# Eight, six and two: a mixture-of-experts kernel whose 16 blocks go through the experts in three groups instead of two

## The chip, the cores and the metric

One core of a Trainium2 chip runs the whole program. The time is device microseconds of one execution; the kernel before has a median of 1375.88 us over 18 runs (1373.22 to 1378.5). A profile is one further execution, with a span of its own.

The engines are named as in the profile: PE is TensorE (PEld its weight loads), DVE is VectorE, ACT is ScalarE, POOL is GpSimd, and SP is the sync engine, which here only issues DMAs.

## What is computed

`x` is 8 sequences of 1024 tokens of 256 numbers, all in float32. Two layers follow each other. The first is an RWKV layer (time mix with a scan over the tokens, then channel mix). The second, which the change is about, sends each token to 4 of 32 experts:

```python
def _L0_ffn_ref(x, expert_sel, keys, values):
    ...
    sel_logits = jnp.einsum('nd,ed->ne', xt, expert_sel)
    gates = jax.nn.sigmoid(sel_logits)
    sel_val, sel_idx = jax.lax.top_k(gates, N_HEADS)
    gate_full = jnp.zeros_like(gates).at[jnp.arange(N)[:, None], sel_idx].set(sel_val)
    scores = jax.nn.relu(jnp.einsum('nd,edf->nef', xt, keys))
    scores = scores * gate_full[:, :, None]
    out = jnp.einsum('nef,efv->nv', scores, values)
    return out.reshape(B, S, -1)
x = L0_attn_x
x = x + _L0_attn_ref(_layernorm(x, axis=-1), L0_attn_ln1_g, ...)
x = x + _L0_ffn_ref(_layernorm(x, axis=-1), L0_ffn_expert_sel, L0_ffn_keys, L0_ffn_values)
return x
```

An expert is a 256x128 matrix, a ReLU and a 128x256 matrix (`N_HEADS` is 4, `E` is 32).

## The kernel before

**Blocks and periods.** The 8192 tokens are 16 blocks of 512, two to a sequence. `period(i)` (L978) is a list of pieces, written out by hand, that works on four blocks at once: the routing of block i-1 (`norm_d`, `apply_d`, `turn_d`, `gates_of`, `rows_of`, `scatter`, `gates_by_row`), the channel mix of block i (`channel`, `channel_end`, which stores the block's result to DRAM as `acc`, L445), the time mix of block i+1, and the load and first norm of block i+2. The loop at L1080 runs periods 0 to 16; in period 16 only the routing of block 15 is left. Between the pieces stand 15 calls of `advance()` (L954).

**Routing.** `gates_of` computes the gates and marks the four largest; `rows_of` gives each token four row numbers in a DRAM buffer `xs` of its group, where each expert has a region of its own. `scatter` puts 16 entries (4 rows of 128 tokens, 4 choices) into the list `waiting`; `post(n)` (L558) issues n of them as indirect DMAs on POOL (L563, `xs<-x,row`, 128 rows each). A helper, `behind_others`, keeps a scatter behind the POOL work written before it.

**Groups.** Blocks are collected into groups, `GROUPS` (L31), before 12 and 4 blocks. When all blocks of a group are routed, its rows can be worked through expert by expert. `expert_group` (L1058) is a generator that does this in small steps beside the periods: `tile_table` counts the rows of each expert and makes a table of tiles; `experts` runs the tiles; `combine` adds the results to the tokens. `advance()` calls `post(1)` and then moves each running generator; the five numbers of a group are its size, the steps to wait before the second half of the table, the tiles per step, the steps between tiles and sums, and the sums per step. A group begins two periods after its last block (L1082), after all that still waits to be scattered is posted at once (L1083). The last group begins after the loop (L1091), and `drain()` calls `advance()` until all is done.

**Tiles.** A tile is 256 rows of one expert; the last 16 tiles of every group are split into two halves of 128 rows for two experts, which is where the partly filled ends of the experts' regions go. So a group of n blocks has `n * 512 * 4 / 256 + 16 = 8n + 16` tiles (`n_tiles`, L148), before 112 and 48. For each tile SP fetches the rows (`xg`, L759), three tiles ahead, five once the periods are over; PE transposes them (`trx`, L794), DVE (in later groups ACT) copies the transposes out (`xgT`, L878) and DVE copies the expert's keys (`key`, L785), PE multiplies by the keys (`ph`, L806), ACT applies the ReLU (`hs`, L884), PE multiplies by the values (`po`, L822), ACT copies that out (`yg`, L888; three buffers, six once the periods are over), and POOL issues two indirect DMAs (`send`, L834, `ys<-yg,to`) that put the rows where their token and choice have their place in DRAM. PE's order is `po` of tile r, `ph` of tile r+2, `trx` of tile r+4.

**Sums.** `combine` handles 128 tokens at a time (a "part", four to a block): SP loads the block's `acc` (`ac`, L901) and gathers 512 KB (`g`, L909), DVE does four multiply-adds (L917), and SP stores the block (L930; the last block part by part, L927). A gather needs every `ys` scatter of its group to have landed. The gathers have two buffers, six once the periods are over; `ac` shares its three buffers (tag `x`) with the blocks that are still under way.

**What sets the order.** A scheduler may move an instruction on its engine where nothing binds it; tiles of a group are pinned to their order, and some norms and loads are kept in program order. Each engine, and each DMA queue, then works through its list in order: SP and POOL stop at an instruction whose input is not there, and everything behind it waits. `clear` fills the front of a group's regions with zeros (two fills of 4224 KB and two of 132 KB on SP's queue); the first is written before the loop, the second after period 0. `load_experts` loads the experts' weights after periods 2 to 5.

Of the kernel before, what the change touches and what calls it, by code (L numbers as in the profile page):

```python
# [27 lines left out]
TS = 256  # L28


GROUPS = ((12, 6, 1.8, 4, 0.8), (4, 4, 1.0, 2, 1.0))  # L31


@with_exitstack
def rwkv_then_routed_experts(
# [43 lines left out]
    groups, first = [], 0  # L79
    for size, *_ in GROUPS:  # L80
        groups.append(list(range(first, first + size)))
        first += size
    assert first == len(blocks)
    group_of = {i: g for g, members in enumerate(groups) for i in members}
# [148 lines left out]
    def transposed(src, c, i, k):  # L233

        ps = ps_a.tile([P, TB], F32, tag="a", name=f"tr_{i}_{k}_{c}")
        for t in range(NT):
            nc.tensor.transpose(ps[:, t * P : (t + 1) * P], src[:, t, c * P : (c + 1) * P], ident)
        return ps
# [109 lines left out]
    def scale_shift(src, i, k):  # L348

        mv = moments(src, i, k)  # L350
        ve = p2.tile([P, NT], F32, tag="ve", name=f"ve_{i}_{k}")
        nc.vector.tensor_scalar(ve, mv[:, :, 1], EPS, None, ALU.add)
        rs = rsqrt(ve, i, k)
        nb = p2.tile([P, NT], F32, tag=f"nb_{k}", name=f"nb_{i}_{k}")
        mine[i][f"{k}_made"] = nc.vector.scalar_tensor_tensor(
            nb, mv[:, :, 0], -1.0, rs, ALU.mult, ALU.mult
        )
        return rs, nb

    def apply(src, dst, rs, nb):  # L360
        for t in range(NT):
            tc.keep_in_program_order(
                nc.scalar.activation(
                    dst[:, t, :D], src[:, t, :], AF.Identity, bias=nb[:, t : t + 1], scale=rs[:, t : t + 1]
                )
            )
# [80 lines left out]
    def norm_d(i):  # L447
        m = mine[i]
        m["d"] = scale_shift(m["x"], i, "d")

    def apply_d(i):
        m = mine[i]
        m["x3"] = p2.tile([P, NT, DX], F32, tag="x3", name=f"x3_{i}")
        apply(m["x"], m["x3"], *m["d"])

    def turn_d(i):
        m = mine[i]
        xT = p3.tile([P, KC, TB], F32, tag="xT", name=f"xT3_{i}")
        for c in range(KC):
            nc.scalar.copy(xT[:, c, :], transposed(m["x3"], c, i, "d"))  # L460
        m["xT3"] = xT

    def gates_of(i):
        m = mine[i]
        xT = m["xT3"]
        ps = ps_a.tile([P, NT, NE], F32, tag="a", name=f"lg_{i}")
        for t in range(NT):
            for c in range(KC):
                nc.tensor.matmul(
                    ps[:, t, :],  # L470
                    xT[:, c, t * P : (t + 1) * P],
                    wsel[:, c, :],
                    start=(c == 0),
                    stop=(c == KC - 1),
                )
        el = p1.tile([P, NT, NE], F32, tag="el", name=f"el_{i}")
        nc.scalar.activation(el, ps, AF.Exp, scale=-1.0)
        nc.vector.tensor_scalar(el, el, 1.0, None, ALU.add)


        ga = p2.tile([P, NT, NE + PAD], F32, tag="ga", name=f"ga_{i}")
        nc.vector.memset(ga[:, :, NE:], -1.0)
        nc.vector.reciprocal(ga[:, :, :NE], el)
        m8 = p2.tile([P, NT, 8], F32, tag="m8", name=f"m8_{i}")
        rp = p1.tile([P, NT, NE + PAD], F32, tag="rp", name=f"rp_{i}")
        for t in range(NT):
            nc.vector.max(m8[:, t, :], ga[:, t, :])
        nc.vector.memset(m8[:, :, TOP:], -1.0)
        for t in range(NT):
            nc.vector.match_replace(rp[:, t, :], m8[:, t, :], ga[:, t, :], -2.0)  # L490
        chosen = p2.tile([P, NT, NE], BF16, tag="chosen", name=f"chosen_{i}")
        nc.vector.tensor_tensor(chosen, ga[:, :, :NE], rp[:, :, :NE], ALU.not_equal)
        m["ga"], m["chosen"] = ga, chosen
# [45 lines left out]
    waiting = []  # L539
    own_names = set()  # L540

    def scatter(i):
        waiting.extend((i, t, k) for t in range(NT) for k in range(TOP))
# [14 lines left out]
    def post(count):  # L558

        for i, t, k in waiting[:count]:  # L560
            m = mine[i]
            g = group_of[i]
            s = nc.gpsimd.indirect_dma_start(  # L563
                out=xs[g],
                out_offset=bass.IndirectOffsetOnAxis(ap=m["row"][:, t, k : k + 1], axis=0),
                in_=m["x3"][:, t, :],
                in_offset=None,
            )
            apart("scatter", g, s)
            behind_others(s)  # L570
        del waiting[:count]

    def gates_by_row(i):

        m = mine[i]
        eq = p2.tile([P, NT, TOP, NE], F32, tag="ek", name=f"eq_{i}")
        gate = keep.tile([P, NT, TOP], F32, name=f"gate_{i}")
        each = [P, NT, TOP, NE]
        nc.vector.tensor_tensor(
            eq,  # L580
            m["key"][:, :, None, :].to_broadcast(each),
            m["k8"][:, :, :TOP, None].to_broadcast(each),
            ALU.is_equal,
        )
        nc.vector.tensor_tensor(eq, eq, m["ga"][:, :, None, :NE].to_broadcast(each), ALU.mult)
        nc.vector.tensor_reduce(gate, eq, AX.X, ALU.add)
        routed[i] = gate
# [363 lines left out]
    total_blocks = len(blocks)  # L951
    background = []

    def advance():  # L954

        post(1)
        for entry in list(background):
            entry[1] += 1.0
            while entry[1] > 0.0:
                try:  # L960
                    entry[1] -= 1.0 / next(entry[0])
                except StopIteration:
                    background.remove(entry)
                    break
# [5 lines left out]
    def beside(stream):  # L970
        next(stream)
        background.append([stream, 0.0])
# [5 lines left out]
    def period(i):  # L978


        do(norm_d, i - 1)
        if i:
            do(mix_wk, i + 1, 0)
        advance()
        do(turn_c, i)
        if i:
            do(mix_vr, i + 1, 0)
        advance()
        do(apply_d, i - 1)
        do(fetch_block, i + 2)  # L990
        do(receptance, i)
        advance()
        do(channel, i, 0)
        if i:
            do(mix_scan, i + 1, 0)
        advance()
        if i:
            do(mix_wk, i + 1, 1)
        do(turn_d, i - 1)
        do(norm_a, i + 2)  # L1000
        advance()
        do(channel, i, 1)
        advance()
        if i:
            do(mix_vr, i + 1, 1)
        advance()
        do(channel, i, 2)
        do(mix_scan, i + 1, 1)
        advance()
        do(gates_of, i - 1)  # L1010
        do(channel, i, 3)
        do(norm_b, i + 2)
        advance()
        do(channel, i, 4)
        advance()
        do(mix_out, i + 1)
        do(norm_c, i + 1)
        advance()
        do(channel, i, 5)
        do(rows_of, i - 1)  # L1020
        do(scatter, i - 1)
        do(turn_b, i + 2)
        advance()
        do(channel, i, 6)
        advance()
        do(channel, i, 7)
        do(gates_by_row, i - 1)
        advance()
        do(apply_c, i + 1)
        do(channel_end, i)  # L1030
        advance()

    STEPS = 16
    norm_a(0)
    norm_b(0)
    turn_b(0)
# [16 lines left out]
    apply_c(0)  # L1053
    mix_scan(1, 0)

    done = set()

    def expert_group(g, wait, tiles, pause, sums):  # L1058

        making = tile_table(g)  # L1060
        next(making)
        for _ in range(wait):
            yield 1.0
        for _ in making:
            pass

        while g and ("tiles", g - 1) not in done:
            yield 1.0
        for _ in experts(g, 0 if g else 4):
            yield tiles  # L1070
        done.add(("tiles", g))
        for _ in range(pause):
            yield 1.0
        while g and ("sums", g - 1) not in done:
            yield 1.0
        for _ in combine(g):
            yield sums
        done.add(("sums", g))

    for i in range(total_blocks + 1):  # L1080
        for g, (size, *pace) in enumerate(GROUPS):
            if i == groups[g][-1] + 2:  # L1082
                post(len(waiting))  # L1083
                beside(expert_group(g, *pace))
        period(i)
        if i + 1 < len(groups):
            clear(i + 1)
        elif 2 <= i < 6:
            load_experts(i - 2)
    blocks_over.append(True)  # L1090
    post(len(waiting))  # L1091
    beside(expert_group(len(groups) - 1, *GROUPS[-1][1:]))
    drain()

# [44 lines left out]
```

## Time and profile before

| what | us |
|---|---|
| median of 18 runs | 1375.88 |
| the profiled execution | 1371.3 |
| its span (the rest lies around it) | 1369.6 |
| PE busy | 1224.6 |
| POOL busy | 636.5 |
| DVE busy | 973.3 |
| ACT busy | 555.9 |
| scatters of rows to `xs` (L563) | 256 of 1000 ns mean |
| scatters of results to `ys` (L834) | 320 of 994 ns mean |
| mean granted TensorE clock | 0.96 |
| bytes moved by DMA | 209.73 MB, mean 153 GB/s |

The span is the time from the first to the last recorded event. [...] "Idle before" an instruction is the time in which its engine did nothing just before it, with what ended that time; "issue" means that nothing that the profile shows was waited for.

### The profile page before, as it was taken

The page shows a single profiled execution, that of the slowest core. Times are in us where ns is not written, and L with a number is a line of the kernel's source. Part 1 is how long each engine was busy: PE and PEld are TensorE (multiplying, and loading weights), DVE is VectorE, ACT ScalarE, POOL GpSimd, SP SyncE. Part 2 cuts the span into 40 slices and gives each one's busy share as a digit, 9 for nine tenths or more (in the row PEclk, how much of TensorE's full clock was granted, in tenths as well). Part 3 has the DMA queues.
Part 4 walks back from the last instruction along what each step waited for, and adds up shares of the span by engine and source line. Part 5 has one row for each costly group of instructions (what it writes and reads, how often), then busy time and mean ns, then how long its engine had stood idle before and what let it go on. Part 6 is the DMA issues. An engine that isn't in the chain of part 4 may idle for free. (4 is left out here: it accounts for less than half of the span.)

```text
span 1369.6 us, 18501 instructions
## 1 busy us (share of the span) xinstructions
PE 1224.6 (89%) x5332; PEld 879.0 (64%) x5332; DVE 973.3 (71%) x3058; ACT 555.9 (41%) x1058; POOL 636.5 (46%) x643
## 2 busy tenths in 40 slices
PE   6999999999999999999999999999998858898800
PEld 2566666666666676666665777878877647676700
DVE  5957878878878879777887765764564645376878
ACT  3354444544544444444544344345343223454400
POOL 2011433432432422523517366677677777777620
PEclk9999999999999999999999999999999989899955
DMA  9900221412401201201203355456566664599999
GB/s 323 342 29 14 87 87 65 152 60 92 152 32 59 91 29 63 91 17 66 85 22 134 101 169 163 141 171 203 165 195 207 192 192 115 216 387 398 347 336 334
DMA packets 119412, 209.73 MB, mean 153 GB/s; under 512 B 17130, under 2 KB 77574, under 8 KB 118800
## 3 DMA queue, kind: packets, MB, share of 16 engines
q1 hardware_dynamic: 89616, 138.71, 32.1%
q0 software_dynamic: 27648, 68.23, 13.5%
q10 hardware_dynamic: 2048, 1.61, 0.4%
q8 instruction: 44, 0.72, 0.2%
q14 instruction: 56, 0.46, 0.1%
HBM read 105.68 MB, written 111.17 MB: 158 GB/s over the span
## 5 line engine op out<-in xcount | busy, mean ns | idle before, releaser
L834 POOL DMA_INDIRECT ys<-yg,to x320 | 318.0, 994 | 146.0 <-issue 56.9
L563 POOL DMA_INDIRECT xs<-x,row x256 | 255.9, 1000 | 83.1 <-issue 63.9
L244 PE MATMUL pj_f<-xT,wkey 128*128 128x512 f32 x512 | 242.2, 596 | 0.8 <-ACT ek L293 0.5
L423 PEld LDWEIGHTS cm<-wval,k 128*128 128x128 f32 x1024 | 194.4, 190 | 73.8 <-issue 49.4
L423 PE MATMUL cm<-wval,k 128*128 128x256 f32 x1024 | 240.4, 379 | 0.1
L806 PE MATMUL ph<-xgT,key 128*128 128x256 f32 (+1 forms) x768 | 173.4, 357 | 36.2 <-ACT hs L884 16.4
L822 PE MATMUL po<-wexp,hs 128*128 x640 | 170.2, 389 | 8.3 <-ACT hs L884 8.1
L371 POOL TENSOR_TENSOR x<-x,xa 128x1024 f32<-128x1024 f32 x16 | 37.7, 2356 | 295.8 <-issue 284.1
L806 PEld LDWEIGHTS ph<-xgT,key 128*128 128x128 f32 x768 | 134.2, 198 | 57.7 <-ACT hs L884 17.0
L878 DVE COPY xgT<-trx 128x512 f32<-128x512 f32 x112 | 76.9, 687 | 128.0 <-PE trx L794 127.7
L917 DVE SCALAR_TENSOR_TENSOR ac<-g,gate,ac 128x256 f32<-128x256 f32 x256 | 121.4, 484 | 44.2 <-DMA g<-ys 39.6
L415 ACT ACTIVATE k<-pj_f 128x512 f32<-128x512 f32 x128 | 76.4, 597 | 186.5 <-PE pj_f L244 186.5
L244 PEld LDWEIGHTS pj_f<-xT,wkey 128*128 128x128 f32 x512 | 92.6, 191 | 71.6 <-issue 66.9
L888 ACT COPY yg<-po 128x512 f32<-128x512 f32 x160 | 93.6, 585 | 89.7 <-DMA ys<-yg,to 89.6
L822 PEld LDWEIGHTS po<-wexp,hs 128*128 128x128 f32 x640 | 113.6, 195 | 25.1 <-ACT hs L884 10.0
L884 ACT ACTIVATE hs<-ph 128x256 f32<-128x256 f32 x160 | 61.9, 387 | 138.3 <-PE trx L794 136.1
L325 DVE RECIPROCAL rw<-rw 128x512 f32<-128x512 f32 x32 | 107.3, 3352 | 1.0
L794 PE MATMUL trx<-ident,xg 128*128 128x128 f32 x640 | 100.4, 280 | 7.7 <-DMA xg<-xs 5.1
L794 PEld LDWEIGHTS trx<-ident,xg 128*128 128x128 f32 x640 | 81.0, 145 | 25.5 <-DMA xg<-xs 7.8
L321 POOL COPY tail<-ek 128x1 f32<-128x1 f32 x16 | 15.7, 982 | 143.5 <-DVE ek L317 141.0
L416 ACT ACTIVATE k<-k 128x512 f32<-128x512 f32 x128 | 80.7, 630 | 4.0
L785 DVE COPY key<-wexp 128x256 f32 x192 | 59.8, 320 | 27.0 <-PE ph L806 12.9
(162 smaller groups left out, 1725.2 us busy)
## 6 DMA issues: line engine op xcount, KB each, us to landing
xg<-xs SPq DMA_DIRECT2D x128, 264.0 KB
g<-ys SPq DMA_DIRECT2D x64, 512.0 KB
xs<-zeros SPq DMA_DIRECT2D x4, 4224.0 KB
xg<-xs SPq DMA_DIRECT2D x64, 132.0 KB
x<-in_x SPq DMA_DIRECT2D x16, 512.0 KB
acc<-x SPq DMA_DIRECT2D x16, 512.0 KB
wexp<-in_w_exp SPq DMA_DIRECT2D x4, 2048.0 KB
ac<-acc SPq DMA_DIRECT2D x16, 512.0 KB
```

Source lines behind the costliest of these rows:

```text
L244: nc.tensor.matmul(ps, w(c), rhs[:, c, :], start=(c == 0), stop=(c == KC - 1))
L325: inverse = nc.vector.reciprocal(rc, rc)
L416: nc.scalar.activation(k2, k2, AF.Square)
L423: nc.tensor.matmul(m["cm"][t // 2][:, t % 2, :], k2[:, t * P : (t + 1) * P], wval[:, f, :], start=(f == 0 and t % 2 == 0), stop=(f == FC - 1),
L563: s = nc.gpsimd.indirect_dma_start(out=xs[g], out_offset=bass.IndirectOffsetOnAxis(ap=m["row"][:, t, k : k + 1], axis=0), in_=m["x3"][:, t ...
L794: nc.tensor.transpose(ps[:, c, j * P : (j + 1) * P], xg[:, j, c * P : (c + 1) * P], ident)
L806: nc.tensor.matmul(ps[:, cols], key[:, c * P : (c + 1) * P], xgT[:, c, cols], start=(c == 0), stop=(c == KC - 1),)
L822: nc.tensor.matmul(ps[:, j, :], hs[:, j * P : (j + 1) * P], wexp[:, bass.ds(e, 1), KC * P :], start=True, stop=True,)
L834: s = nc.gpsimd.indirect_dma_start(out=ys[g], out_offset=bass.IndirectOffsetOnAxis(ap=to[:, j : j + 1], axis=0), in_=yg[:, j, :], in_offse ...
L878: after(move(xgT, trx), signal)
L888: after(nc.scalar.copy(yg, po), signal)
L917: nc.vector.scalar_tensor_tensor(ac, gk, routed[i][:, t, k : k + 1], ac, ALU.mult, ALU.add)
```

## The change

`GROUPS` gets three entries: 8, 6 and 2 blocks, with 80, 64 and 32 tiles and paces of their own. There is a third `clear`, after period 1, and a third tile table. Period 16 is replaced by `closing(15)`, which does the routing of block 15 with three calls of `advance()` instead of 15. A group that begins no longer posts all waiting scatters at once: `expert_group` notes that it has begun, `advance()` then posts two a step while the first waiting entry is of such a group, and the tiles wait until none of the group's is left.

```diff
-GROUPS = ((12, 6, 1.8, 4, 0.8), (4, 4, 1.0, 2, 1.0))
+GROUPS = ((8, 6, 1.1, 4, 0.8), (6, 4, 2.0, 4, 1.0), (2, 1, 1.0, 2, 1.0))
...
     def advance():
 
-        post(1)
+        post(2 if waiting and group_of[waiting[0][0]] in begun else 1)
         for entry in list(background):
...
-    STEPS = 16
+    def closing(i):
+
+        norm_d(i)
+        post(2)
+        advance()
+        apply_d(i)
+        post(2)
+        advance()
+        turn_d(i)
+        gates_of(i)
+        post(2)
+        advance()
+        rows_of(i)
+        scatter(i)
+        gates_by_row(i)
+
...
-    done = set()
+    done, begun = set(), set()
 
     def expert_group(g, wait, tiles, pause, sums):
 
+        begun.add(g)
         making = tile_table(g)
         next(making)
         for _ in range(wait):
             yield 1.0
         for _ in making:
             pass
+
+        while any(group_of[i] == g for i, _, _ in waiting):
+            yield 1.0
 
         while g and ("tiles", g - 1) not in done:
             yield 1.0
...
     for i in range(total_blocks + 1):
         for g, (size, *pace) in enumerate(GROUPS):
             if i == groups[g][-1] + 2:
-                post(len(waiting))
                 beside(expert_group(g, *pace))
+        if i == total_blocks:
+            closing(i - 1)
+            break
         period(i)
...
     blocks_over.append(True)
-    post(len(waiting))
     beside(expert_group(len(groups) - 1, *GROUPS[-1][1:]))
     drain()
```

## The prediction

> **What bounds the kernel now.** I read the page's forty slices first, then the stretches, then the waits and the order of time where one stretch hands over to the next.
>
> ```profile
> PE   6999999999999999999999999999998858898800
> POOL 2011433432432422523517366677677777777620
> DMA  9900221412401201201203355456566664599999
> ```
>
> A slice is 34.24 us. Up to about 1027 us PE is full; after that it has gaps, POOL stays at 6 to 7 tenths, and DMA fills up at the end. The stretches say what the 7 means (columns: busy time and count of PE, PEld, DVE, ACT, POOL, then TensorE clock, DMA share, GB/s):
>
> ```profile
> 411.00:445.00 34.00, 34.00 (x131) 22.00 (x130) 27.98 (x77) 16.76 (x30) 9.36 (x11) 1.00 0.17 59
> 1061.00:1096.00 35.00, 28.05 (x143) 22.91 (x141) 22.30 (x106) 9.36 (x22) 26.99 (x27) 0.95 0.66 193
> 1233.00:1267.00 34.00, 27.20 (x152) 21.79 (x151) 23.29 (x84) 16.20 (x36) 26.03 (x26) 1.00 1.05 399
> 1335.00:1370.00 35.00, 0.00 (x0) 0.00 (x0) 27.90 (x62) 0.00 (x0) 0.00 (x0) 0.50 0.90 327
> ```
>
> 27 scatters in 35 us is one per 1.30 us, of which 1.00 is busy. The waits of POOL show that the rest isn't a wait for anyone:
>
> ```profile
> POOL ys L834 <- issue: 27.1, 89, 0.3
> POOL xs L563 <- issue: 8.5, 28, 0.3
> ```
>
> (1013 to 1268 us; total, times, longest.) 0.3 us lies between any two scatters, so 1.28 us a scatter is POOL at its limit, and a tile (two scatters) costs 2.56 us there. On PE a tile costs less:
>
> ```profile
> 1038.11 1.03 PE L822 MATMUL po<-wexp,hs 128*128 x4
> 1038.97 1.03 PE L806 MATMUL ph<-xgT,key 128*128 128x256 f32 x4
> 1039.83 0.60 PE L794 MATMUL trx<-ident,xg 128*128 128x128 f32 x4
> 1040.27 1.03 PE L822 MATMUL po<-wexp,hs 128*128 x4
> ```
>
> From one `po` to the next 2.165 us: 0.87 for `po`, 0.87 for `ph`, 0.43 for `trx`. So the kernel is PE-bound while blocks run, POOL-bound from there to the last scatter (1310.6 us), and then sums only: 1311.9 to 1369.6, 57.7 us.
>
> ```profile
> 515.62 0.37 SPq L445 DMA_DIRECT2D acc<-x  x1
> 568.44 0.37 SPq L445 DMA_DIRECT2D acc<-x  x1
> 1182.68 6.15 DMA g<-ys
> 1341.69 24.80 DVE L917 SCALAR_TENSOR_TENSOR ac<-g,gate,ac 128x256 f32<-128x256 f32 x52 [0.15 <-DMA g<-ys]
> ```
>
> The first two (SP's queue) give the period without tiles, 52.82 us. The third (the chain of waits) prices a gather. The last is the final stretch of sums, 13 parts in 24.8 us: 1.91 a part.
>
> **Part 1, the sizes.** 8n+16 tiles a group makes 80+64+32 = 176 for 160: 16 tiles more, or 34.6 us on PE (16 x 2.165) and 41.0 on POOL (32 x 1.28). The third fill (8.9 MB) follows the second on SP; two took SP from 12.0 to 64.5 us, so this one ends near 91, before block 0's store at 93.2 and the load at 101.3 that are behind it, and the DMA share from 68 to 103 us was 0.10. It costs 0; without that cover, up to 5. Also at 0, behind POOL's limit in part 4: the third table (three small products and some 45 small DVE operations), `xgT` on ACT for 96 tiles in place of 48 (ACT then has 0.585 + 0.385 + 0.585 = 1.56 us a tile against POOL's 2.56), and `closing`, whose 12 lost steps move tiles of group 1 behind block 15's routing but not their number; with POOL not full, each of the three would cost PE a few us at a group's start, as at 1054.3 us, where PE sat 2.9 us before block 15's gates.
>
> **Part 2, to the end of group 0.** In the changed kernel's instruction order all 80 tiles of group 0 stand inside periods 9 to 14, none before. Block 8's store is unchanged at 515.6. Six periods are 316.9, 80 tiles 173.2: block 14's store at 1005.7. Group 0's start cost something before: the period from 727.5 to 808.5 us took 81.0, where 52.8 and 12 `trx`, 10 `ph`, 9 `po` (21.7) explain 74.5. I take 4 of those 6.5 us (bounds 0 and 6.5), since the burst of scatters is gone. POOL has room: 16.5 tiles a period and 16 row scatters are 49 x 1.28 = 63 us, with the other POOL operations of a period (2.4 for x, 2 x 1.3 for the tails) 68 of 88.5. A store is 2.3 us behind PE's last product, and the last `po` of group 0 stands 1.7 before that end: call it T = 1006.
>
> **Part 3, group 1's start.** Here the "two by two" doesn't happen. Group 0's last tile ends a period before group 1 begins, so in POOL's order there is nothing left to put between: its last two scatters, two rows of block 12 and all 16 of block 13 stand in one run, 20 x 1.28 = 26 us, to T+27. They land (2.4 us, `xs<-x,row` rows of the chain), SP fetches (753.63 to the first `trx` at 756.57: 2.9), so `trx` of tile 0 starts at T+33. PE has period 15 to do until then, but not freely: DVE's first sums of group 0 stand in its order before the end of the table and of block 14's norm. They wait for the gather of rows just scattered (two scatters, landing, 6.15: T+12) and for another that needs its buffer (T+20); PE then has 11 us to the tile. It arrives at T+33 too.
>
> Behind it SP's order is: fetch 0, a gather, fetch 1, a load, fetch 2, two gathers, the store of block 0, **the load of block 2, which waits until that store has landed**, fetch 3. From T+30: gather 6, sums 1.9 and what DVE has between, T+40; store 5 (1.5 us for 524 KB at 340 GB/s, 11.94 the longest `out<-ac` of the chain): T+46; fetch 3 at T+49. In PE's order the fourth `trx` is ahead of the first `po`; that, and ACT's copy of 0.6, bring POOL its first result scatter at T+51. POOL stands idle for 24 us. Without the wait of SP it would be T+41 (7.8 us of PE work and the copy after `trx`), idle 14; with the longest store T+58, idle 31. Before, POOL crossed its group change without such a gap, because tiles of group 0 were still queued behind the burst.
>
> [...]
>
> **Part 4, POOL to its last scatter.** 96 tiles are 192 scatters, blocks 14 and 15 add 32. Undisturbed 1.28; with sums beside them, 65 between 1183.1 and 1267.8 us, 1.32. At 1.31 they take 293 us; I add 7, about the two waits before 1274 and 1278 us in the trace (4.9 and 1.2). From T+51 that is T+351 = 1357, where before it was 1311.9. Here the two by two does happen, for block 15, and is worth nothing: POOL is full with or without the mixture. PE, from T+33, needs 208 us for 96 tiles and some 20 for the rest of period 15 and block 15's routing: T+261, so POOL covers it, and would cover waits of PE in the closing chain of several tens of us.
>
> [...]
>
> **Part 5, the end.** Before, 26 gathers were still to come when PE ended; now group 1's 24 parts run beside group 2's 32 tiles and 8 parts remain. Landing 2.5, a gather 6, eight parts 15.3, last store 3.1 (last sum 1366.5, end 1369.6): 27. I take 31, for what group 1 leaves over; bounds 25 and 42.
>
> **The sum.** 1357 + 31 = 1388 of span, 18 more than 1369.6: POOL's last scatter comes 45 later (41 for added scatters; the rest is the gap, less what was done earlier), the end is 27 shorter. The profiled run lies 4.6 below the median, so 1375.9 + 18 = **1394 us**. Lower bounds together (no start loss, idle 14, 1.30 a scatter, end 25): 1002 + 41 + 291 + 25 = 1359, or 1365 on the median's scale; upper bounds 1008 + 58 + 305 + 42 = 1413, or 1419.
>
> **Rivals.**
> - *The gap closes (20%).* If group 0's tiles in fact lag on POOL, so that its run of scatters covers the table and the fetch, POOL never idles: 1006 + 244 x 1.29 + 31 = 1352, 1358 on the median's scale, faster. For it: the trace crosses the change at 1130 us with PE idle for 16.4 us and POOL full. Against: 20 us of slack a period in part 2. It decides from a gap below some 6 us.
> - *DMA takes over at the end (12%).* A part moves 0.79 MB (gather, load, store) and a tile 0.53. Group 2's phase has one part a tile, 36 MB: at 387 GB/s 93 us, against 82 on POOL; with SP's waits for stores 10 to 20 us more: 1404 to 1414. For it: 1233 to 1267 at 399 GB/s. Against: POOL was full there all the same.
> - *Shorter end and added tiles cancel (8%).* With the gap near 10: 1374 to 1379.
> - The change not doing what it says is part 3, and already in the forecast.
>
> The forecast has 60%. Likeliest range 1380 to 1408. About 0.2% (2.8 us) is what can be told from no change. Faster has the first rival and a little, 21%; within 0.2% 7%; slower 72%. The range goes from the first rival's 1358 to the second's 1414.
>
> **What would show it.** Right: 352 result scatters; block 14's store near 1010; 16 row scatters without a break just after, then POOL idle over 15 us; last scatter near 1357; about 30 us from there to the end. Wrong: a gap of a few us, scatters at more than 1.4 us, an end beyond 45, or tiles that stretch the periods by more than 2.165 each.

## The result, and the profile after

| | before | after |
|---|---|---|
| median, us | 1375.64 (50 runs) | 1392.75 (8 runs, 1390.86 to 1394.25) |
| ratio to before | | 1.0125, 95% interval 1.0114 to 1.0136 |
| span of the profiled execution | 1369.6 | 1390.6 |
| block 14's store, block 15's store | 919.59, 1013.55 | 1010.67, 1091.29 |
| scatters not yet begun at block 15's store | 225 | 204 |
| end of POOL's last scatter | 1311.8 | 1368.6 |
| from there to the end | 57.8 | 22.1 |

The changed kernel is 17 us slower. The last four rows are the account used for every run below: a span is block 15's store (up to there PE sets the pace), plus the scatters that are left times the time of one, plus the end. Before it is 1013.6 + 225 x 1.325 + 57.8, after it is 1091.3 + 204 x 1.359 + 22.1. The store comes 77.7 us later, POOL's part is 20.9 shorter, the end 35.8 shorter: 21.0 us of span. That is 4 us more than the medians differ by, because the profiled execution of the kernel before was one of its quicker ones (1371.3 us, its median 1375.6); the one after was at its median (1392.3). Spans of single executions, in this section and the next, are to be read with that much room.

The forty slices of the page, now 34.77 us each:

```profile
PE   6999999999999999999999999999978888796881
POOL 2011343333333334356565555555653777777762
DMA  9990231421411212244434435333167999754995
```

POOL's 3 in the slice at 1043 us, between a 5 and the 7s, is the hole of the prediction's part 3. Its two edges, in POOL's order of time (start, duration, operation, and in brackets the idle time before it and who ended that):

```profile
1031.30 0.96 POOL L563 DMA_INDIRECT xs<-x,row  x1 [0.30 <-issue]
1061.09 1.00 POOL L834 DMA_INDIRECT ys<-yg,to  x1 [28.83 <-ACT yg L888]
```

The run of row scatters ends at 1032.3 us, and POOL is idle for 28.83 us until a result of group 1 is ready. The chain that ended last goes through the same stretch. Its longest pieces there (start, duration):

```profile
1007.80 2.42 DMA ys<-yg,to
1010.25 4.13 DMA g<-ys
1017.07 7.27 DMA g<-ys
1028.99 5.10 PE pj_f L244 x8
1034.86 6.11 DMA xg<-xs
1043.14 6.12 DMA out<-ac
1049.84 4.00 DMA xg<-xs
1055.06 1.81 PE po L822 x4
```

Read downwards: group 0's last result lands, two gathers for its sums follow, then products for block 15's mix on PE, a fetch of group 1's first rows, **the store of block 0's result**, and only behind it one more fetch. SP's order shows the hold:

```profile
1010.67 0.40 SPq L445 DMA_DIRECT2D acc<-x  x1
...
1043.14 0.43 SPq L930 DMA_DIRECT2D out<-ac  x1
1049.28 0.37 SPq L901 DMA_DIRECT2D ac<-acc  x1
1049.84 0.97 SPq L759 DMA_DIRECT2D xg<-xs  x2
```

The load of block 2 starts 6.1 us after the store, when that has landed (6.12 in the chain), and the fourth fetch of rows stands behind it. What the two gathers do to PE is seen on DVE and PE:

```profile
1020.41 0.15 DVE L229 SCALAR_TENSOR_TENSOR step_d<-step_d,rs_d 128x4 f32<-128x4 f32 x1
1024.37 0.48 DVE L917 SCALAR_TENSOR_TENSOR ac<-g,gate,ac 128x256 f32<-128x256 f32 x1 [3.80 <-DMA g<-ys]
1024.77 0.21 DVE L230 SCALAR_TENSOR_TENSOR rs_d<-step_d,rs_d 128x4 f32<-128x4 f32 x1
1024.90 0.47 DVE L917 SCALAR_TENSOR_TENSOR ac<-g,gate,ac 128x256 f32<-128x256 f32 x1
1025.30 0.15 DVE L355 SCALAR_TENSOR_TENSOR nb_d<-mv_d,rs_d 128x4 f32<-128x4 f32 x1
```

```profile
1017.00 1.46 PE L423 MATMUL cm<-wval,k 128*128 128x256 f32 x6
1026.18 2.80 PE L237 MATMUL tr_d<-ident,x 128*128 128x128 f32 x8 [7.72 <-ACT x L363]
1028.78 5.29 PE L244 MATMUL pj_f<-xT,wkey 128*128 128x512 f32 x8
...
1053.97 1.09 PE L794 MATMUL trx<-ident,xg 128*128 128x128 f32 x4 [6.46 <-DMA xg<-xs]
1054.85 2.02 PE L822 MATMUL po<-wexp,hs 128*128 x4
```

Between two steps of block 14's norm (`step_d`, then `rs_d`, `nb_d`) stands a sum that waits 3.80 us for its gather. So `nb_d` comes at 1025.30, ACT applies the norm, and PE, whose next instruction in order needs it, has waited 7.72 us. Later it waits 6.46 us for the fetch behind SP's hold. After each wait its matmuls are slower: the eight `pj_f` take 5.29 us where eight took 3.6 a period earlier, and after the second wait `po` takes 2.02 for 1.03 (last section).

The scatters themselves cost nearly what they did before, from the page's groups:

```profile
L834 POOL DMA_INDIRECT ys<-yg,to x352 | 354.6, 1007 | 264.9 <-ACT yg L888 180.2
```

352 for 320, 1007 ns for 994. The end, from the chain: one gather after the last scatter has landed, and sums.

```profile
1367.58 2.42 DMA ys<-yg,to
1370.01 3.76 DMA g<-ys
1383.63 3.66 DVE ac L917 x9
```

### The profile page after: what moved, and what is told of

The parts are those of the page before. It is cut to its first block, busy times and chain, and to the rows that moved or that the text cites. A ratio compares the mean times of both kernels' runs of the same rounds, so it can differ in the third digit from the quotient of the medians.

```text
span 1390.6 us, 19448 instructions
## 1 busy us (share of the span) xinstructions
PE 1273.4 (92%) x5590; PEld 919.9 (66%) x5590; DVE 957.6 (69%) x3150; ACT 594.0 (43%) x1138; POOL 674.7 (49%) x678
## 4 chain that ended last, share of the span: by engine, by line
PE 71%; DMA 12%; DVE 7%; issue 4%; POOL 3%; ACT 1%; SPq 1%; DVEq 0%; POOLq 0%; ACTq 0%
PE pj_f L244 15%; PE cm L423 14%; PE ph L806 6%; PE po L822 6%; DMA g<-ys 4%; PE tm L338 4%; DMA ys<-yg,to 4%; PE pj_v L244 4%; PE pj_r L244 3%; PE pj_w L244 3%; PE trx L794 3%; PE pj_k L244 3%; PE rec L397 3%; DVE ac L917 2%; POOL ys L834 2%
## 5 line engine op out<-in xcount | busy, mean ns | idle before, releaser
L834 POOL DMA_INDIRECT ys<-yg,to x352 | 354.6, 1007 | 264.9 <-ACT yg L888 180.2
L806 PE MATMUL ph<-xgT,key 128*128 128x256 f32 (+1 forms) x896 | 192.1, 347 | 21.4 <-DVE key L785 7.5
L822 PE MATMUL po<-wexp,hs 128*128 x704 | 190.2, 394 | 3.0 <-ACT hs L884 1.8
L806 PEld LDWEIGHTS ph<-xgT,key 128*128 128x128 f32 x896 | 152.5, 198 | 45.0 <-issue 21.5
L917 DVE SCALAR_TENSOR_TENSOR ac<-g,gate,ac 128x256 f32<-128x256 f32 x256 | 119.8, 481 | 68.9 <-DMA g<-ys 56.4
L822 PEld LDWEIGHTS po<-wexp,hs 128*128 128x128 f32 x704 | 129.9, 198 | 27.8 <-issue 12.8
L794 PE MATMUL trx<-ident,xg 128*128 128x128 f32 x704 | 111.7, 284 | 24.3 <-ACT xgT L878 14.8
L888 ACT COPY yg<-po 128x512 f32<-128x512 f32 x176 | 102.9, 585 | 65.1 <-DMA ys<-yg,to 61.5
L785 DVE COPY key<-wexp 128x256 f32 x224 | 71.8, 327 | 77.2 <-PE ph L806 64.6
L878 DVE COPY xgT<-trx 128x512 f32<-128x512 f32 x80 | 54.5, 681 | 88.1 <-PE trx L794 87.8
L878 ACT COPY xgT<-trx 128x512 f32<-128x512 f32 x96 | 56.2, 588 | 111.1 <-PE trx L794 110.2
L416 ACT ACTIVATE k<-k 128x512 f32<-128x512 f32 x128 | 80.6, 630 | 4.1
```

Source lines behind the costliest of these rows:

```text
L416: nc.scalar.activation(k2, k2, AF.Square)
L794: nc.tensor.transpose(ps[:, c, j * P : (j + 1) * P], xg[:, j, c * P : (c + 1) * P], ident)
L806: nc.tensor.matmul(ps[:, cols], key[:, c * P : (c + 1) * P], xgT[:, c, cols], start=(c == 0), stop=(c == KC - 1),)
L822: nc.tensor.matmul(ps[:, j, :], hs[:, j * P : (j + 1) * P], wexp[:, bass.ds(e, 1), KC * P :], start=True, stop=True,)
L834: s = nc.gpsimd.indirect_dma_start(out=ys[g], out_offset=bass.IndirectOffsetOnAxis(ap=to[:, j : j + 1], axis=0), in_=yg[:, j, :], in_offse ...
L878: after(move(xgT, trx), signal)
```

## The experiments

The numbers of all runs, by the account above (in the profiled execution; the ratio is to the kernel before, from timed runs):

| run | store of 15 | left | us each | end | span | ratio (95%) |
|---|---|---|---|---|---|---|
| before (12, 4) | 1013.6 | 225 | 1.325 | 57.8 | 1369.6 | |
| after (8, 6, 2) | 1091.3 | 204 | 1.359 | 22.1 | 1390.6 | 1.0125 (1.0114, 1.0136) |
| e1_groups_only | 1122.4 | 183 | 1.360 | 22.1 | 1393.4 | 1.0150 (1.0135, 1.0166) |
| e2_posting_only | 992.7 | 248 | 1.363 | 57.2 | 1387.9 | 1.0069 (1.0056, 1.0083) |
| e3_slow_96 | 1073.7 | 209 | 1.389 | 21.7 | 1385.9 | 1.0097 (1.0082, 1.0113) |
| e4_late_sums | 1091.7 | 205 | 1.361 | 22.1 | 1392.9 | 1.0140 (1.0125, 1.0156) |
| e5_16_more_g1 | 1015.0 | 257 | 1.313 | 39.0 | 1391.4 | 1.0128 (1.0111, 1.0145) |
| e8_norm_first | 1088.1 | 203 | 1.363 | 21.9 | 1386.6 | 1.0099 (1.0082, 1.0116) |
| e7_10_4_2 | 1027.7 | 242 | 1.345 | 22.1 | 1375.2 | 1.0035 (1.0020, 1.0049) |
| b_10_4_2 | 1053.6 | 230 | 1.355 | 23.8 | 1389.0 | 1.0132 (1.0115, 1.0149) |
| e9_10_4_2_norm | 1026.8 | 242 | 1.358 | 21.9 | 1377.4 | 1.0035 (1.0022, 1.0047) |
| e10_two_10_6 | 1041.7 | 201 | 1.367 | 57.9 | 1374.4 | 0.9994 (0.9985, 1.0003) |
| e11_before_10_6 | 1055.6 | 188 | 1.425 | 56.4 | 1379.9 | 1.0045 (1.0031, 1.0059) |
| e12_10_6_pace | 1088.2 | 154 | 1.493 | 57.4 | 1375.5 | 0.9998 (0.9987, 1.0008) |

### Which half of the change: sizes alone, posting alone

e1_groups_only is the kernel before with the new sizes; e2_posting_only is the changed kernel with the old ones.

```diff
e1_groups_only, against before:
-GROUPS = ((12, 6, 1.8, 4, 0.8), (4, 4, 1.0, 2, 1.0))
+GROUPS = ((8, 6, 1.1, 4, 0.8), (6, 4, 2.0, 4, 1.0), (2, 1, 1.0, 2, 1.0))
e2_posting_only, against after:
-GROUPS = ((8, 6, 1.1, 4, 0.8), (6, 4, 2.0, 4, 1.0), (2, 1, 1.0, 2, 1.0))
+GROUPS = ((12, 6, 1.8, 4, 0.8), (4, 4, 1.0, 2, 1.0))
```

> The kernel before with the three groups 8, 6 and 2 and their paces, but with the old posting (all waiting row scatters at once when a group begins) and period 16 as it was. Theory A (POOL is the limit once the blocks are over; the change loses by 32 added result scatters and by the gap at group 1's start, wins by the shorter end, and the posting and the closing piece are worth nothing): 1387 to 1398 us, with 15 us or more of POOL gap at group 1's start. Rival B (the posting and the closing piece, with 3 steps instead of 15 beside block 15's routing, carry the loss): 1380 or less.

> The changed kernel with the groups and paces of before (12 and 4 blocks): the new posting and the closing piece alone. Theory A: within 4 us of before (1372 to 1380), since POOL is full on both sides of the group change either way. Rival B: 1385 or more.

Sizes alone cost 20 us (1395.9 us), posting and closing alone 10 (1385.6). The first was expected, the second not: with the old sizes it should have been neutral. Together they cost 17, so with the new sizes posting and closing give back 3. A reading of why it costs with 12 and 4: the scatters of rows are put off from a time when POOL has room to one when it has none. Before 740 us the kernel before has begun 79 of the 472 scatters that start after 500 us, e2 71; at 1250 us it has 42 left, e2 52. And from 1240 to 1300 us POOL waits, counting waits over 1 us, for 12.1 us in five places where before it waited 6.1 in two (4.88 and 1.24). The three longest in e2:

```profile
1270.42 1.04 POOL L834 DMA_INDIRECT ys<-yg,to  x1 [3.90 <-ACT yg L888]
1273.51 0.98 POOL L834 DMA_INDIRECT ys<-yg,to  x1 [2.04 <-DVE key L785]
1291.90 0.98 POOL L834 DMA_INDIRECT ys<-yg,to  x1 [3.71 <-ACT yg L888]
```

Ten scatters at 1.3 are 13 us and the waits add some 5 (less 0.3 a place that is there anyway), of the 19.0 by which POOL ends later. But these two executions lie 18 us apart and the medians 9.6 (e2's profiled one was its slowest, 1389.6, the one before a quick one), so this account explains more than the change costs, and some of these waits may be the execution's own. Which of the two functions (posting, closing) costs the 10 us was not separated.

### Sixteen more tiles in the kernel before

e5_16_more_g1 gives the last group of the kernel before 16 more tiles. They are dead: their places lie past the last row, so they fetch spare rows and scatter nothing of use; PE, ACT and POOL do the work of a tile for them.

```diff
-        n_tiles.append(gt * TOP // TS + NE // 2)
+        n_tiles.append(gt * TOP // TS + NE // 2 + (16 if g == 1 else 0))
```

> The kernel before with 16 more tiles in its last group (64 instead of 48); no rows fall into them, so they fetch spare rows and scatter nothing, but every instruction of a tile is there. It prices 16 tiles by themselves. Theory A (after the last block's store POOL sets the pace): 32 scatters at 1.28 to 1.36 us, 41 to 44 us more, 1416 to 1420. Rival (PE sets it): 16 x 2.165 = 35, 1411. Rival (other work covers them): below 1396.

1392.95 us: by the ratio 17.6 more, instead of 41 or more. POOL paid the full price: its last scatter ends at 1352.4, 40.6 us later, 1.27 for each of 32. But the end shrank from 57.8 to 39.0, because DVE's sums ran beside the added scatters. Multiply-adds of L917 (busy time and count of DVE in each stretch), first in e5, then in the kernel before:

```profile
1352.00:1391.00 39.00, 28.72 (x64) 0.50 0.81 296
```

```profile
1312.00:1369.00 57.00, 45.81 (x99) 0.50 0.95 338
```

64 are left after POOL's last scatter in e5, 99 before. So the end is a backlog of sums that any longer POOL phase eats into, and a tile in the last phase costs nearer 1.1 us of time (17.6/16) than 2.56 as long as that backlog lasts. In the changed kernel that backlog is gone: eight parts of the last group, which need the last scatter, are all that is left.

### The start of group 1: pace, sums, norm

Three edits of the changed kernel, one each.

```diff
e3_slow_96 (group 0's tiles a step), e4_late_sums (group 0's steps between tiles and sums):
-GROUPS = ((8, 6, 1.1, 4, 0.8), (6, 4, 2.0, 4, 1.0), (2, 1, 1.0, 2, 1.0))
+GROUPS = ((8, 6, 0.96, 4, 0.8), (6, 4, 2.0, 4, 1.0), (2, 1, 1.0, 2, 1.0))
+GROUPS = ((8, 6, 1.1, 22, 0.8), (6, 4, 2.0, 4, 1.0), (2, 1, 1.0, 2, 1.0))
e8_norm_first, DVE's order only, for group 0's first sum and group 1's first place computation:
+    def behind_norm(ins):
+        tc.add_manual_dep(
+            ins.ins,
+            mine[14]["d_made"].ins.name,
+            mybir.DependencyInfo(mybir.DependencyClass.NoSync, mybir.DependencyReason.DATA),
+            reason="the norm goes first",
+        )
...
+            if g == 1 and t == 0:
+                behind_norm(first)
...
+                if g == 0 and j == 0 and k == 0:
+                    behind_norm(one)
```

> The changed kernel with one number changed: group 0 runs 0.96 tiles a step instead of 1.1, so that its last tiles lie beside group 1's row scatters and table. Theory A: POOL's 28.8 us gap before group 1's first result scatter falls below 8 and the time falls by 16 to 28, to 1365 to 1377. Rival C (the gap is covered: PE's or DMA's total work sets the end anyway): within 5 us of the changed kernel's 1392.75.

> The changed kernel with one number changed: group 0's sums begin 22 steps after its tiles instead of 4, so that neither DVE nor SP holds a sum, a gather or a store of group 0 in front of group 1's first tiles. Theory A: PE's waits of 7.7 and 6.5 us there go, the gap on POOL falls from 28.8 to 13 to 18 us (row scatters, landing, fetch and first tile remain), the time falls by 8 to 15, to 1378 to 1385, if the later sums don't lengthen the end. Rival C: no change. Rival D (transfers bound the last 150 us): the later sums push traffic to the end, 1395 or more.

> The changed kernel with two order edges on DVE: group 0's first sum and group 1's first place computation come after block 14's last norm step. Theory A: PE's wait of 7.7 us before block 14's transposes goes, but PE then reaches group 1's first tile before its rows (33 us after the last tile of group 0), so it waits up to 10 us there: 0 to 8 us faster than 1392.75, 1385 to 1393. Rival E (the order on DVE is the whole of the 24 us that PE loses in period 15): 1368 to 1376.

**e3**: 1388.72 us, 4 less than the changed kernel; the expectation of 16 to 28 less fell. The hole did close, its largest pieces on POOL are now

```profile
1047.18 1.23 POOL L563 DMA_INDIRECT xs<-x,row  x1 [7.14 <-DVE order L774]
1055.41 1.00 POOL L834 DMA_INDIRECT ys<-yg,to  x1 [5.74 <-ACT yg L888]
```

and block 15's store comes 17.5 us earlier. But five more scatters are left there, and one costs 1.389 instead of 1.359: POOL's phase takes 13.1 us longer. So the hole's 28.83 us can't be taken as a term of the sum by itself: PE, which is what bounds the kernel up to block 15's store, did period 15's work during most of it.

**e4**: 1394.88 us, where 1378 to 1385 was expected: 2 more than the changed kernel instead of 8 to 15 less. All but one of the sums left that stretch, and the store of block 0 with them, but another wait took their place on DVE, one step ahead of the norm's last operations; DVE, then PE:

```profile
1036.86 0.17 DVE L766 TENSOR_TENSOR later<-xg,limit 128x8 f32<-128x8 f32 x1 [18.95 <-DMA xg<-xs]
```

```profile
1038.04 2.16 PE L237 MATMUL tr_d<-ident,x 128*128 128x128 f32 x8 [19.08 <-ACT x L363]
```

Group 1's first place computation waits for its fetch, which waits for the row scatters, and block 14's norm is queued behind it. That led to **e8**, which puts both kinds behind the norm: 1388.43 us, inside what was expected. PE's wait at `tr_d` falls from 7.72 to 2.42:

```profile
1021.71 0.33 PE L246 MATMUL tr_d<-ident,x 128*128 128x128 f32 x1 [2.42 <-ACT x L372]
```

and block 15's store comes 3.2 us earlier. (Its lines are numbered 9 higher here, and up to 11 further on.) SP's hold went too: here the fourth fetch goes out at 1045.37 us, ahead of the store of block 0 at 1049.92, and PE's second wait falls from 6.46 to 2.62. POOL's hole is still 23.04 us. DVE's order at group 1's start, with what SP does behind it, is thus worth about 4 us.

### Other sizes, three groups and two

The same two programs with 10, 4 and 2 blocks (16 more tiles, as 8, 6 and 2), with e8's edit added, and with 10 and 6 blocks (no added tiles).

```diff
e7_10_4_2 (after), b_10_4_2 (before), e9_10_4_2_norm (e8):
+GROUPS = ((10, 6, 1.2, 4, 0.8), (4, 4, 2.0, 4, 1.0), (2, 1, 1.0, 2, 1.0))
e10_two_10_6 (after), e11_before_10_6 (before):
+GROUPS = ((10, 6, 1.3, 4, 0.8), (6, 4, 1.0, 2, 1.0))
e12_10_6_pace (after):
+GROUPS = ((10, 6, 1.8, 4, 0.8), (6, 4, 1.0, 2, 1.0))
```

> The changed kernel with groups of 10, 4 and 2 blocks (176 tiles too), so that tiles of group 0 still run when group 1 begins. By theory A with the accounts of the runs so far: block 15's store at 868 + 71 tiles x 2.165 + 5 = 1027, some 244 scatters left at 1.36 = 332, end 22: span 1381, 1386 us (1380 to 1392). Rival (the gap at group 1's start is what costs): 1370 or less, since there is none.

> The same groups of 10, 4 and 2 with the old posting and the old period 16. More tiles stand ahead of block 15's store: 868 + 77 x 2.165 + 5 = 1040, some 231 scatters left at 1.34 = 310, end 22: span 1372, 1377 us (1371 to 1384). So the posting and the closing piece would cost about 9 us here, as with the groups of before. Rival (the posting is worth nothing): equal to the run with the new posting within 4 us.

> The changed code with groups of 10, 4 and 2 blocks, and with group 0's first sum and group 1's first places put behind block 14's norm in DVE's order (the two edits of the earlier runs together). Theory (the norm's delay costs about 4 us wherever group 0's sums begin beside block 14's routing, and adds to the gain of the other sizes): 1379.5 - 4 = 1374 to 1377, no difference from before. Rival (with ten blocks in group 0, group 1 begins when tiles of group 0 are still queued, no gap and no early sums, so there is nothing for the norm to gain): 1378 to 1381.

> The changed code with two groups of 10 and 6 blocks: 160 tiles as before, group 0's 96 tiles all ahead of block 15's store. If the 16 added tiles are what the change loses by, this has none of them: the store of block 15 some 40 tiles later (1013.6 + 40 x 2.165 = 1100), some 145 scatters left at 1.33 (1293), an end of 50 to 58 us as before: 1345 to 1355, with the loss at a group's start of up to 24 us 1355 to 1375 on the median's scale: at least as fast as before. Rival (what costs is a group that begins with the one before it done, whatever the number of tiles): the loss comes back, scatters wait, 1376 to 1392.

> The code of before with the same two groups of 10 and 6 blocks. Theory (the way of posting and the closing piece are worth something where group 0 is done early, as with 10, 4 and 2: 13 us, and cost where tiles of group 0 are left over, as with 12 and 4: 10 us): 5 to 13 us slower than the changed code with 10 and 6. Rival (their worth comes with the third group only): within 3 us of it.

> The changed code with two groups of 10 and 6 blocks and 1.8 tiles a step in group 0 instead of 1.3. With 1.3, 201 scatters were left at block 15's store (1041.7), where 128 + 32 would be left had group 0's tiles all been ahead of it: some 20 tiles of group 0 ran behind it. Theory (a tile moved ahead of the store costs 2.165 us on PE and saves 2 x 1.367 on POOL): 20 x 0.57 = 11 us less, 1361 to 1367, faster than both kernels. Rival (group 0 done before group 1's table brings back the gap on POOL and the waits of PE at the group's start, up to 24 us): 1372 to 1387.

**e7**: 1379.54 us, 13 less than with 8, 6 and 2, the best of all three-group versions and 5 more than before. Group 0's tiles are still queued on POOL when group 1 begins, so there is no hole; all of POOL's waits for results from 950 to 1180 us (total, times, longest), to be held against the 28.83 above:

```profile
POOL ys L834 <- ACT yg L888: 9.0, 8, 2.4
```

By the account it does 19 tiles fewer ahead of block 15's store (38 more scatters left). At 2.165 that is 41 us of PE, but its store comes 63.6 earlier: 22.5 us of PE were lost in the changed kernel, as much as its waits and slow matmuls in period 15 add up to (16.3 + 6.4, in the section after this). POOL's phase is 48.1 longer, and what is left of the 63.6 is the 15.4 between the spans. **e9** adds nothing to it (1379.77), as its rival said: with no hole there are no early sums to hold up the norm.

**b_10_4_2** missed, 1392.59: the new posting and closing are worth 13 us with these sizes, where they were worth 3 with 8, 6, 2 and cost 10 with 12, 4. **e11** against e10 gives 7 us for two groups, in the middle of what was expected, so it isn't the third group that makes them useful. In b against e7 the store of block 15 comes 25.8 us later. Six tiles more ahead of it are 13.0 of that, and the trace shows where most of the rest comes from. The burst of row scatters that the old posting puts in one run stands on POOL in front of the two scatters of a result. ACT's next copy of a result waits 12.10 us until those have landed and a buffer is free, `k` is behind the copy in ACT's order, and PE waits 9.73 us for `k` (POOL, ACT, PE; e7 has no wait of PE over 2.5 us between 500 us and that store):

```profile
989.38 1.00 POOL L834 DMA_INDIRECT ys<-yg,to  x1 [0.30 <-DMA xs<-x,row]
993.22 0.58 ACT L888 COPY yg<-po 128x512 f32<-128x512 f32 x1 [12.10 <-DMA ys<-yg,to]
993.70 0.60 ACT L415 ACTIVATE k<-pj_f 128x512 f32<-128x512 f32 x1
994.36 0.37 PE L702 MATMUL tr_say<-ident,scratch 128*4 128x128 f32 x1 [9.73 <-ACT k L415]
```

So here posting two by two pays, while PE sets the pace, by avoiding that wait; the 12 scatters fewer behind the store give b back 13.8. In e11 against e10 the store comes 13.8 later, which is its 6.5 tiles more; the 13 scatters fewer should give back 17.8 and give 6.9, mostly because POOL waits more behind the store: beyond the 0.3 us between any two scatters, 19.1 us in seven places where e10 has one wait of 12.1.

**e10**: 1374.43 us, the same as before (0.9994). That is at the edge between the theory with a loss at the group's start (1355 to 1375) and the rival (1376 to 1392), so it doesn't decide between them; the range of 1345 to 1355 without a loss at the start was far off. It has a stall of its own, PE at the start of group 1, behind block 15's routing:

```profile
1137.42 2.07 PE L794 MATMUL trx<-ident,xg 128*128 128x128 f32 x8 [38.45 <-DMA xg<-xs]
```

**e12** tried to use that: more tiles of group 0 ahead of block 15's store. 1374.89 us; the rival held. 47 scatters fewer are left at the store, which comes 46.5 us later, and then POOL has nothing to do until group 1's first result:

```profile
1111.16 1.37 POOL L563 DMA_INDIRECT xs<-x,row  x1 [9.66 <-issue]
1149.11 1.16 POOL L834 DMA_INDIRECT ys<-yg,to  x1 [16.92 <-ACT yg L888]
```

In both, group 1's first result reaches POOL at 1148 to 1149 us. No version tried is faster than the kernel before by what can be measured.

## Why the prediction was right

The forecast of 1394 us, slower, came out within 1.3 us of the median, and the rivals (the gap closes, DMA takes over, the two cancel) did not happen. Part of that closeness is luck: POOL's last scatter came 11.6 us later than predicted and the end was 8.9 shorter, and the forecast added 6.3 us from span to median, as in the kernel before, where the changed kernel's two lie 2.1 apart, which makes up for the 2.6 by which the span came out longer.

| step | predicted | measured |
|---|---|---|
| part 2, block 14's store | 1010 | 1010.67 |
| part 2, group 0's last `po` (T) | 1006 | 1005.5 |
| part 3, POOL idle | 24 (14 to 31) | 28.83 |
| part 3, group 1's first result scatter | 1057 (T+51) | 1061.1 |
| part 4, from there to the last scatter, 224 scatters | 300 (1.34 each) | 307.5 (1.373 each) |
| part 4, last scatter | 1357 | 1368.6 |
| part 5, the end | 31 (25 to 42) | 22.1 |
| span | 1388 | 1390.6 |

**Part 1** held: no wait appeared at the third fill, and e5 priced the added tiles on POOL at 1.27 us a scatter for the 1.28 taken. **Part 2** held to the microsecond, so the 4 us for group 0's start were about right. **Part 3** held in its mechanism, shown line by line in the chain: a run of row scatters without a break, sums of group 0 in DVE's order ahead of the norm, the store of block 0 holding SP's fetch for 6.1 us. Up to the fourth fetch its times held as well: the second gather, with the norm behind it, was expected at T+20 and landed at T+18.8, the fetch was expected at T+49 and landed at T+48.3. Its size was 4.8 short, and all of that lies in the last step: from the landed fetch to POOL's first result it allowed 2 us, and it took 7.2. PE ran its share at a granted clock of 0.50 (last section), and ACT, which copies `xgT` too in the later groups, had the first result's copy (at 1060.22) in its order behind the next tile's `xgT`, for which it waited 3.50 us. (The prediction took 6 us for a gather and 5 for the store; the two gathers of the chain took 4.13 and 7.27 us there, the store 6.12.) What it gave no price is what the same waits do to PE, though it had the norm held up until T+20. PE stood 7.72 and 6.46 us, and with smaller waits 16.3 in period 15, and its matmuls after each wait were slow (`tr_d` 2.80 for 1.04 a period earlier, the eight `pj_f` 5.29 for 3.6, then `trx`, `po` and `ph` 3.0 over: together 6.4). Blocks 14's and 15's stores lie 80.6 us apart where the period's work and its tiles come to some 57.5 (its matmuls, counted at the pace of the periods before). It cost the forecast nothing, because its chain ran over POOL and not over block 15's store.

**Part 4** was mis-sized: 1.373 us a scatter, not 1.34. POOL's waits for a result from 1061 us to its last scatter (total, times, longest):

```profile
POOL ys L834 <- ACT yg L888: 47.3, 20, 28.8
```

Without the hole that is 18.5 us in 19 waits; 0.3 us lies between any two scatters, so 12.8 us are waits proper, where 7 were allowed. That is 5.8 of the 7.5; the rest is 1.315 us a scatter for 1.31 (294.7 / 224), and rounding. The step that failed in part 4 is that the two by two "is worth nothing": e1, e2, and the pairs with 10, 4, 2 and 10, 6 put it and the closing piece, which were only run together, at 3 us here, at minus 10 with the old sizes, and at 13 and 7 with the others. Taken as 0 it was a small error for this change alone.

**Part 5** was mis-sized the other way by 9: the gather took 3.76 for 6, the eight parts 14.0 for 15.3 (1373.8 to 1387.8), the last scatter had landed 1.4 after POOL was done with it, for 2.5, and group 1 left nothing over, where 4 were allowed. The late last scatter and the short end are one thing: the longer POOL's phase, the more of the sums lie beside it, as e5 showed.

**The answer to where it went.** By the account, 16 more tiles cost POOL 41 us and the shorter end gives back 36, so three groups as such should lose about 5. That is what e7 and e9 lose; it is an account that fits, not a separate experiment. Two groups with the same code lose nothing with 10 and 6 blocks (e10), but 10 us with 12 and 4 (e2). The other 12 to 13 us belong to the sizes 8, 6, 2, as e7 shows: group 0 is done a period before group 1 starts, PE loses 22.5 us in period 15, and part of that is regained because more tiles are done ahead of the store. e8 gets 4 of it by DVE's order (SP's hold goes with it), e3 4 by the pace. So cutting PE's two waits from 14.2 to 5.0 us, as e8 does, gets back a third; POOL's hole of 23 us stays in e8. What would get the rest with these sizes, and whether e3 and e8 add up, stays open.

The sum has no term for the copies of keys that the added tiles bring to DVE, and the trace shows little to pay for them. A copy takes 327 ns. The scatters' mean went from 994 to 1007 ns, with 352 scatters and 224 copies (192 before); the 150 scatters that lay beside a copy took 1017 ns, the other 202 took 1000.

## What to carry to other kernels

A group more costs its padding on the engine that is full (here 41 us on POOL by the account), and gives back only what the last group's tail cost (here 36 us); compute both before cutting a tail, and remember that the tail shrinks by itself when the phase before it grows (in e5 from 57.8 to 39.0 us). An idle gap on one engine is not a term of the time (in e3 POOL's 28.83 us fell to waits of 7.14 at most, for 4 us of time): look at what the bounding engine did in it, and at what a wait in one engine's order (here a sum ahead of a norm) holds up on the next. Spread work out only from a time when its engine is full to one when it has room; the same edit gained 13 us or lost 10, by what stood behind the scatters that it moved.

## What the hardware showed

PE's two waits of 7.72 and 6.46 us in period 15 cost more than their own length. Stretches of the changed kernel (columns as in the stretches before: after busy times and counts of five engines, the granted TensorE clock):

```profile
1024.00:1027.50 3.50, 1.28 (x3) 0.55 (x3) 1.96 (x6) 1.97 (x4) 2.59 (x3) 0.50 0.25 92
1027.50:1031.00 3.50, 3.48 (x9) 2.14 (x9) 0.00 (x0) 1.28 (x3) 2.88 (x3) 0.50 0.32 116
1031.00:1034.50 3.50, 3.50 (x9) 1.63 (x8) 0.00 (x0) 1.62 (x3) 0.96 (x1) 0.83 0.21 77
1034.50:1038.00 3.50, 3.50 (x25) 3.11 (x24) 0.63 (x3) 1.11 (x3) 0.00 (x0) 1.00 0.85 276
...
1052.00:1055.50 3.50, 1.53 (x6) 1.34 (x7) 0.79 (x5) 0.41 (x1) 0.00 (x0) 0.59 0.99 309
1055.50:1060.00 4.50, 4.50 (x15) 3.69 (x14) 2.99 (x12) 1.00 (x4) 0.00 (x0) 0.56 0.63 248
1060.00:1064.00 4.00, 4.00 (x18) 2.79 (x17) 2.12 (x11) 2.73 (x7) 2.30 (x3) 1.00 0.52 119
```

After the wait of 7.72 us PE works from 1026.2 to about 1032 at a clock of 0.50, after that of 6.46 from 1054 to about 1059.5, and then at 1.00: 6.0 and 5.5 us of work at half clock after the two waits. The trace has the clock of 0.50 from 1021.94 to 1032.18 and from 1052.66 to 1059.48 us, 10.24 and 6.83 long and 20.48 apart; both times it began during the wait. In this case 14.2 us of waiting were followed by matmuls that took 6.4 us longer.
